# First adder convolution: three near slots and a gathered list per 32 positions, in place of four slots and one list per 128

## The chip, the cores and the metric

The kernel runs on one core of a Trainium2 chip. A core has a matrix engine (TensorE, "PE" in the profile, with its weight loads listed apart as "PEld"), a vector engine (VectorE, "DVE"), an activation engine (ScalarE, "ACT"), a general engine (GpSimd, "POOL") and a queue engine that starts most transfers (SyncE, "SP"). Each engine works through its own list of instructions in order and waits on semaphores for the others.

The metric is the device time of one execution in microseconds. It was 13987.03 us before the change, the median of three runs (13982.17 to 13997.77). One further execution was recorded by the profiler: 13941.95 us, with a span of 13939.6 us from its first to its last instruction.

## The reference, cut to what matters

The whole computation is four layers on an image batch of 4 x 128 x 64 x 64. The change lies in layer 1, in the first of its two adder convolutions:

```python
def adder_conv(x, w):                 # 3x3, stride 1, pad 1
    patches = lax.conv_general_dilated_patches(x, (3, 3), (1, 1), [(1, 1), (1, 1)])
    p = patches.reshape(N, Ck, H * W)                  # Ck = 128 * 9
    def per_channel(wc):
        return -jnp.sum(jnp.abs(p - wc[None, :, None]), axis=1)
    out = lax.map(per_channel, w.reshape(Cout, Ck))
    ...
out = adder_conv(shift_conv(x, w_shift1), w_add1)
out = relu(batchnorm(out))
out = adder_conv(shift_conv(out, w_shift2), w_add2)
```

So every output is a sum of 1152 absolute differences between values y of the shift convolution and weights w. Layer 0 (an attention over 4096 positions) comes before it, layers 2 and 3 after it.

## The kernel before

**What is summed.** An absolute difference is rewritten as |y - w| = 2 relu(w - y) + y - w. For one input channel and one position the term 2 relu(w - y) is a row of 1152 numbers (9 taps x 128 output channels). If y lies above all weights of the channel, the row is zero. If it lies below all of them ("below"), the row is linear in w and y. Only in between ("near") must the row be formed. For each group of 128 positions (there are 128 groups, numbered m; four of them make a block q of 512 positions) the rows are summed over channels into a 128 x 1152 tile `t` of three PSUM banks:

- `add_linear` (L600): nine bf16 matmuls for the "below" values, three for each bank.
- Near slots: in every window of 32 positions, slot l holds for each channel its l-th near position. `distance` forms r = relu(w + at) for the 128 channels, 128 x 1152, on VectorE (L575) or ScalarE (L573), taking turns. `add_near` (L585) multiplies it by a one-hot matrix `hot_n` of 32 columns. The four windows g of a group go to the four 32-column strips of the array; there are 12 such matmuls for a slot, and an f32 matmul is two records in the profile. `S_NEAR` is 4.
- The list: near values that found no slot are listed for the whole group, up to 8 for a channel (`TOP`) and up to 128 in all, each in a seat (a partition) of its own. An indirect DMA on GpSimd's queue, `weights_of` (L522), gathers for each seat the weight row of its channel (128 rows of 4608 bytes) into a tile `wl` of the pool `gp` (three buffers). One `distance` and one `add_far` (L592, three matmuls of 128 columns) add it.
- A group whose list overflows is marked in `crowded` and left to `sparse_rest`, a loop whose number of passes is read from the data. The trace before holds no instruction of this loop's own lines (L808, L815).

**Closing.** `closed` (L610) copies the three banks out on ScalarE to `tsa`; `combine` (L633) adds them into the output with shift matmuls on TensorE. Both are issued one group late: after slot l = 1 of the next group.

**Preparing the next block.** While the groups of block q are summed, a generator `found(q + 1)` prepares block q + 1 in small steps. Its parts in order: the shift convolution (L297, nine taps, with the casts of L288 and L289 for the block after), `ranks` (L418 to L427), `totals` (matmuls of L557, result read by VectorE at L564), `slots` (L538 to L542), and `listed`: counts (L451 to L461), two matmuls for the seats (L464, L465), `max` and `max_index` for each stretch (L468, L469), `chairs` (a 0/1 matrix of seats, L480), the fields `what` (L485 to L495), the list matmuls (L500), eight empty steps (`AFTER`), and `value`, `lanes`, `hot` (L508 to L515). After every `distance` a call of `beside` advances the generator by 88 / 68 steps (68 distances in a block).

**What sets the order.** Nearly all these instructions are held in the program's order (`keep_in_program_order`), so the order of the emission is the order on each engine. What may run ahead is set by buffers: r has six for VectorE (`r0`) and six for ScalarE (`r1`), and PSUM has five banks for `t`, three of which a group takes.

Of the kernel before, what the change touches and what calls it, by code (L numbers as in the profile page):

```python
# [9 lines left out]
F32 = mybir.dt.float32  # L10
BF16 = mybir.dt.bfloat16
# [3 lines left out]
ALU = mybir.AluOpType  # L15
AX = mybir.AxisListType
# [3 lines left out]
P = 128  # L20
# [5 lines left out]
BK = 512  # L26
# [273 lines left out]
        ))  # L300


S_NEAR, TOP, FIELDS = 4, 8, 5
AFTER = 8
FAR = 2.0 ** 100
GROUPS = BK // P
# [3 lines left out]
class Sparse:  # L310
# [85 lines left out]
    def pools(self, ctx, r_bufs):  # L396
        def pool(name, bufs, **kw):
            return ctx.enter_context(self.tc.tile_pool(name=f"{self.tag}{name}", bufs=bufs, **kw))

        self.tp = pool("t", 1)  # L400
        self.kp = pool("q", 2)
        self.rp = pool("r", r_bufs)
        self.lp = pool("l", 1)
        self.gp = pool("g", 3)
        self.op = pool("o", 2)
        self.ps_t = pool("pt", 5, space=PSUM)
        self.ps_o = pool("po", 2, space=PSUM)
        self.ps_c = pool("pc", 1, space=PSUM)
        self.banks = {}
        self.begun = set()  # L410
        self.evacuated = {}
# [30 lines left out]
    def listed(self, q, v, near, counts):  # L442

        nc, then, u = self.tc.nc, self.tc.keep_in_program_order, f"{self.tag}{q}"
        small, data = [P, GROUPS], [P, GROUPS, TOP]

        def new(shape, name, dtype=F32):
            return self.lp.tile(shape, dtype, tag=name, name=f"{name}{u}")

        away = self.tp.tile([P, BK], F32, tag="t1", name=f"away{u}")  # L450
        then(nc.vector.tensor_scalar(away, near, S_NEAR + 0.5, -FAR, ALU.is_lt, ALU.mult))  # L451
        yield
        masked = self.tp.tile([P, BK], F32, tag="t3", name=f"masked{u}")
        then(nc.vector.tensor_tensor(masked, away, v, ALU.add))
        yield
        count = new(small, "count")
        then(nc.vector.tensor_reduce(count, away.rearrange("p (j k) -> p j k", k=P), AX.X, ALU.add))
        then(nc.vector.tensor_scalar(count, count, 1.0 / FAR, float(P), ALU.mult, ALU.add))
        full = new(small, "full")
        then(nc.vector.tensor_scalar(full, count, float(TOP), 1000.0, ALU.is_gt, ALU.mult))  # L460
        then(nc.vector.tensor_tensor(full, full, count, ALU.add))  # L461
        yield
        pb = self.ps_c.tile([P, 2, GROUPS], F32, tag="cv", name=f"pbase{u}")
        then(nc.tensor.matmul(pb[:, 0, :], self.before, full, start=True, stop=False, skip_group_check=True))  # L464
        then(nc.tensor.matmul(pb[:, 1, :], self.cm.ones, full, start=False, stop=True, skip_group_check=True))  # L465
        at, where = new(data, "at8"), new(data, "where", U32)
        for j in range(GROUPS):
            then(nc.vector.max(at[:, j, :], masked[:, bass.ts(j, P)]))  # L468
            then(nc.vector.max_index(where[:, j, :], at[:, j, :], masked[:, bass.ts(j, P)]))  # L469
            yield  # L470
            yield
        crowded = self.crowded[:, GROUPS * q : GROUPS * (q + 1)]
        then(nc.vector.tensor_scalar(crowded, pb[:, 1, :], float(P), None, ALU.is_gt))
        base = new(small, "base")
        then(nc.vector.scalar_tensor_tensor(base, crowded, 1000.0, pb[:, 0, :], ALU.mult, ALU.add))
        then(nc.vector.tensor_tensor(counts[:, GROUPS * q : GROUPS * (q + 1)], crowded, count, ALU.mult))
        yield
        wide = [P, GROUPS, TOP + P]
        chairs = self.lp.tile(wide, BF16, tag="chairs", bufs=2, name=f"chairs{u}")
        then(nc.vector.tensor_tensor(  # L480
            chairs, self.chair.unsqueeze(1).broadcast_to(wide), base.unsqueeze(2).broadcast_to(wide), ALU.is_equal
        ))
        yield
        valid = new(data, "valid")
        then(nc.vector.tensor_scalar(valid, at, -FAR / 2, None, ALU.is_gt))  # L485
        then(nc.vector.tensor_tensor(at, at, valid, ALU.mult))
        what = new([*data, FIELDS], "what", BF16)
        then(nc.vector.tensor_copy(what[..., 0], at))
        yield
        then(nc.vector.tensor_tensor(at, at, what[..., 0], ALU.subtract))  # L490
        then(nc.vector.tensor_copy(what[..., 1], at))
        then(nc.vector.tensor_tensor(what[..., 2], at, what[..., 1], ALU.subtract))
        yield
        then(nc.vector.scalar_tensor_tensor(what[..., 3], where, 1.0, valid, ALU.add, ALU.mult))
        then(nc.vector.tensor_scalar(what[..., 4], valid, self.lane, None, ALU.mult))  # L495
        yield
        pl = self.ps_c.tile([P, GROUPS, FIELDS], F32, tag="cv", name=f"plist{u}")
        for j in range(GROUPS):
            for l in range(TOP):
                then(nc.tensor.matmul(  # L500
                    pl[:, j, :], chairs[:, j, TOP - l : TOP - l + P], what[:, j, l, :], start=(j + l == 0),
                    stop=(j == GROUPS - 1 and l == TOP - 1), skip_group_check=True,
                ))
            yield
        for _ in range(AFTER):
            yield
        value, of = self.kp.tile(small, F32, tag="value", name=f"value{u}"), new([P, GROUPS, 2], "of")
        then(nc.vector.tensor_reduce(value, pl[:, :, 0:3], AX.X, ALU.add))  # L508
        then(nc.vector.tensor_copy(of, pl[:, :, 3:5]))
        lanes = self.kp.tile(small, I32, tag="lanes", name=f"lanes{u}")  # L510
        then(nc.vector.tensor_copy(lanes, of[:, :, 1]))
        yield
        hot = self.kp.tile([P, GROUPS, P], F32, tag="hotl", name=f"hotl{u}")
        for j in range(GROUPS):
            then(nc.vector.tensor_scalar(hot[:, j, :], self.place, of[:, j, 0:1], 2.0, ALU.is_equal, ALU.mult))  # L515
        yield
        yield value, lanes, hot

# [124 lines left out]
def sparse_adder(tc, cm, sp, x_d, wqs, stats, counts, p_d, y_d, tag):  # L643
# [7 lines left out]
    nc = tc.nc  # L651
    then = tc.keep_in_program_order
    with ExitStack() as ctx:
# [76 lines left out]
            pass  # L730
        groups = blocks * GROUPS
        waiting = None
        per = (S_NEAR * 4 + 1) * GROUPS

        ripe = []

        def combined(m, t, total):
            b, n = divmod(m, N // P)
            sp.combine(b, n, sp.closed(t, m, total))
            ripe.extend([AFTER, b, k] for k in sp.done(n))  # L740

        steps, due = iter(()), 0.0
        for m in range(groups):
            q, j = divmod(m, GROUPS)
            if j == 0:
                for _ in steps:
                    pass
                below, total, hot_n, at_n, value, lanes, hot_l = ready.pop(q)
                steps = found(q + 1) if q + 1 < blocks else iter(())

            def beside(of):
                nonlocal due
                for waits in list(ripe):
                    waits[0] -= 1
                    if waits[0] == 0:
                        finished(*waits[1:])
                        ripe.remove(waits)
                due += of * 88.0 / per
                while due >= 1.0:
                    due -= 1.0  # L760
                    next(steps, None)

            t = sp.open_rows(m)
            weights = sp.weights_of(lanes[:, j : j + 1], m)
            sp.add_linear(t, below[:, bass.ts(j, P)])
            for l in range(S_NEAR):
                rs = []
                for g in range(4):
                    w = 4 * j + g
                    rs.append(sp.distance(g % 2 == 1, at_n[:, l, w : w + 1], f"n{m}_{l}_{g}"))  # L770
                    beside(1)
                sp.add_near(t, lambda g: hot_n[:, l, P * j + 32 * g : P * j + 32 * g + 32], lambda g: rs[g], False)
                if l == 1 and waiting is not None:
                    combined(*waiting)
            r = sp.distance(m % 2 == 1, value[:, j : j + 1], f"l{m}", weights)
            beside(1)
            sp.add_far(t, hot_l[:, j, :], r, False, True)
            waiting = (m, t, total[:, j : j + 1])
        combined(*waiting)
        for _, b, k in ripe:  # L780
# [1945 lines left out]
```

## Time and profile before

| what | before |
|---|---|
| median of three runs | 13987.03 us |
| profiled execution, its time and its span | 13941.95 us, 13939.6 us |
| TensorE, VectorE, ScalarE, GpSimd busy over the span | 91%, 77%, 66%, 31% |
| first adder convolution, from the first group to the last result | 2050 to 4238 us |
| in it TensorE, VectorE, ScalarE, GpSimd busy, of 2188 us | 2114, 1479, 1519, 180 us |
| granted TensorE clock in it | 0.99 |
| one block of four groups (two successive first gathers, 2994.32 to 3062.97 us) | 68.65 us |

A row of a group of instructions gives line, engine and operation, the tile written and the tiles read, their shapes and how many there were; after the bar the busy time and the mean of one; after the second bar how long the engine was idle just before them and who ended that. A row of the timeline gives start and length in us, with the idle time before it in square brackets. A row of the windows gives, for a stretch of time, the busy time and number of instructions of TensorE, its weight loads, VectorE, ScalarE and GpSimd, then the granted clock, the share of the DMA engines and GB/s.

### The profile page before, as it was taken

The numbers are of one execution on the slowest core, as the hardware profiler recorded it, in microseconds if no ns is written. First come the engines' busy times: TensorE is split into PE (matmuls) and PEld (weight loads), VectorE is DVE, ScalarE is ACT, GpSimd is POOL, SyncE is SP. The second block draws the span as 40 slices with busy tenths as digits, with TensorE's granted clock in tenths as the row PEclk, the third lists the DMA queues.
The fourth block names the chain that finished last, engine by engine and source line by source line (L and its number), as shares of the span: only waits on it lengthen the run. The fifth ranks groups of instructions, "written<-read, shape, count | busy, mean of one in ns | idle before, by whom it ended". The sixth has DMA issues, their size and how long they took to land. (4 is left out here: it accounts for less than half of the span.)

```text
span 13939.6 us, 217437 instructions
## 1 busy us (share of the span) xinstructions
PE 12715.4 (91%) x85293; PEld 5605.6 (40%) x85320; DVE 10711.0 (77%) x15704; ACT 9244.1 (66%) x10490; POOL 4389.7 (31%) x2328
## 2 busy tenths in 40 slices
PE   9999989999996999999999999997788869899998
PEld 4444434444443334334533454444233223333332
DVE  7778876666664778777777778875786689999997
ACT  5666646666664788877787778884333456676676
POOL 5666640000001001001000100001000159999997
PEclk9999989999997999999999999998887679999999
DMA  0000001111111101101100211114110368999997
GB/s 17 10 5 11 5 22 47 47 49 49 48 45 47 37 33 39 38 27 59 61 30 24 71 55 51 52 54 124 19 17 35 123 205 235 247 255 254 252 256 200
DMA packets 388839, 1134.70 MB, mean 81 GB/s; under 512 B 143317, under 2 KB 171792, under 8 KB 315980
## 3 DMA queue, kind: packets, MB, share of 16 engines
q1 hardware_dynamic: 322332, 857.60, 21.1%
q0 software_dynamic: 65312, 260.86, 6.2%
q8 instruction: 676, 11.08, 0.3%
q14 instruction: 375, 3.07, 0.1%
q10 hardware_dynamic: 144, 2.10, 0.0%
HBM read 910.21 MB, written 202.38 MB: 80 GB/s over the span
## 5 line engine op out<-in xcount | busy, mean ns | idle before, releaser
L573 ACT ACTIVATE ra<-a2wa,vc 128x1152 f32<-128x1152 f32 x2397 | 2875.6, 1250 | 661.8 <-PE ta L1264 648.2
L1264 PE MATMUL ta<-ra,a2pick 128*32 128x384 f32 x33024 | 3174.1, 494 | 104.6 <-DVE ra L575 63.8
L575 DVE TENSOR_SCALAR ra<-a2wa,vc 128x1152 f32<-128x1152 f32 x3107 | 2425.3, 818 | 766.6 <-PE ta L1264 751.6
L2387 PE MATMUL mg<-h,ident 128*128 128x512 f32 x4096 | 1957.8, 616 | 206.6 <-ACT m L2396 168.5
L1264 PEld LDWEIGHTS ta<-ra,a2pick 128*32 128x32 f32 x33024 | 1310.0, 110 | 1623.2 <-issue 852.2
L2372 DVE TENSOR_TENSOR_SCAN h<-da,h,dbu 128x1024 f32<-128x1024 f32 x768 | 1804.4, 2349 | 128.8 <-ACT da L2358 37.4
L573 ACT ACTIVATE ra1n<-a1wa,atna 128x1152 f32<-128x1152 f32 x1024 | 1227.2, 1248 | 601.5 <-PE ta L585 584.7
L2387 PEld LDWEIGHTS mg<-h,ident 128*128 128x128 f32 x4096 | 727.7, 191 | 1438.4 <-ACT m L2396 690.1
L190 POOL TENSOR_TENSOR ssum<-ssum,et 128x512 f32<-128x512 f32 x960 | 1228.8, 1280 | 233.3 <-ACT et L185 166.6
L2400 POOL TENSOR_TENSOR m<-m,C 128x2048 f32<-128x2048 f32 x256 | 1157.1, 4532 | 102.0 <-ACT m L2396 81.6
L2351 POOL TENSOR_TENSOR dbu<-du,B 128x2048 f32<-128x2048 f32 x256 | 1157.2, 4535 | 100.1 <-DMA B<-xdbl_d 45.1
L575 DVE TENSOR_SCALAR ra1n<-a1wa,atna 128x1152 f32<-128x1152 f32 x1024 | 806.3, 814 | 419.7 <-PE ta L585 400.7
L585 PE MATMUL ta<-ra1n,hotna 128*32 128x384 f32 x12288 | 1089.4, 489 | 12.9 <-DVE ra1n L575 12.9
L522 POOL DMA_INDIRECT wla<-in_w_add,lanes x156 | 173.9, 1115 | 2940.6 <-DVE lanes L1235 1375.5
L1264 PE MATMUL ta<-ra,hot 128*32 128x384 f32 x10368 | 1046.9, 498 | 53.9 <-ACT ra L573 36.1
L153 PE MATMUL pe<-q,k 128*128 128x512 f32 x2048 | 1051.1, 596 | 8.7 <-DVE mx L163 8.1
L196 PE MATMUL pav<-et,vT 128*128 128x512 f32 x2048 | 1042.0, 593 | 1.5 <-ACT et L185 1.5
L573 ACT ACTIVATE ra<-a2wa,at 128x1152 f32<-128x1152 f32 x793 | 944.4, 1248 | 131.8 <-PE ta L1264 125.4
L155 ACT COPY et<-pe 128x512 f32<-128x512 f32 x1024 | 595.4, 581 | 592.3 <-PE pe L153 575.7
L163 DVE TENSOR_TENSOR mx<-pe,mx 128x512 f32<-128x512 f32 x992 | 679.6, 685 | 336.0 <-ACT et L155 332.9
L575 DVE TENSOR_SCALAR ra<-a2wa,at 128x1152 f32<-128x1152 f32 x935 | 728.9, 817 | 224.8 <-PE ta L1264 221.1
L2358 ACT ACTIVATE da<-dl,af 128x1024 f32<-128x1024 f32 x512 | 572.6, 1118 | 420.5 <-DVE h L2372 325.7
(486 smaller groups left out, 16692.2 us busy)
## 6 DMA issues: line engine op xcount, KB each, us to landing
dl<-delta_d SPq DMA_DIRECT2D x256, 512.0 KB
dl<-delta_d SPq DMA_DIRECT2D x512, 256.0 KB
du<-du_d SPq DMA_DIRECT2D x256, 512.0 KB
du<-du_d SPq DMA_DIRECT2D x512, 256.0 KB
taps_d<-tsa SPq DMA_DIRECT2D x82, 576.0 KB
sz_d<-sz SPq DMA_DIRECT2D x64, 256.0 KB
xs_d<-xs SPq DMA_DIRECT2D x8, 2048.0 KB
delta_d<-dv SPq DMA_DIRECT2D x32, 512.0 KB
```

The source lines that it names most:

```text
L153: nc.tensor.matmul(pe, k[:, bass.ts(j, P)], unit[u, "q"], start=True, stop=True)
L163: nc.vector.tensor_tensor(mx, pe, mx, ALU.max)
L190: nc.gpsimd.tensor_tensor(unit[u, "sum"], unit[u, "sum"], at, ALU.add)
L196: nc.tensor.matmul(unit[u, "av"], image[u // NB][2][:, j, :], at, start=(j == 0), stop=(j == NJ - 1))
L573: then(nc.scalar.activation(r, w, AF.Relu, bias=at))
L575: then(nc.vector.tensor_scalar(r, w, at, 0.0, ALU.add, ALU.max))
L585: self.tc.keep_in_program_order(self.tc.nc.tensor.matmul(t[y][32 * g : 32 * g + 32, :], lhs(g), rhs(g)[:, bass.ts(y, TC)], start=first, st ...
L1264: self.tc.keep_in_program_order(self.tc.nc.tensor.matmul(t[y][32 * g : 32 * g + 32, :], lhs, r[:, bass.ts(y, TC)], start=first, stop=False ...
L2351: then(nc.gpsimd.tensor_tensor(t, du, by_states(tiles[n][0], 0, h), ALU.mult))
L2372: then(nc.vector.tensor_tensor_scan(t[:, cols][:, s], da[:, s], st[n, "dbu", h][:, cols][:, s], 0.0 if e % 4 == 0 else st["last"], ALU.mul ...
L2387: then(nc.tensor.matmul(pm, cm.ident, st[n, way, h][:, bass.ts(k, BK)], start=(way == 0), stop=(way == 1)))
L2400: then(nc.gpsimd.tensor_tensor(m, m, by_states(tiles[n][0], 1, h), ALU.mult))
```

## The change

The near slots go from four to three. The list is made for each window of 32 positions in place of each 128: a block has 16 lists (`WINDOWS`) of up to 128 seats in place of four. Each group gathers four weight tiles in place of one, forms four distances from them (two on each engine), and adds them with `add_near`, in the form of a slot, in place of `add_far`. The gather pool has six buffers in place of three; `chairs` has one in place of two. `beside` advances the generator by 104 / 64 steps (64 distances in a block). `crowded` is still kept for each group of 128: a group is marked if any of its four lists overflows.

```diff
@@ -300,7 +300,8 @@
         ))
 
 
-S_NEAR, TOP, FIELDS = 4, 8, 5
+S_NEAR, TOP, FIELDS = 3, 8, 5
+WINDOWS = BK // 32
 AFTER = 8
 FAR = 2.0 ** 100
 GROUPS = BK // P
@@ -401,7 +402,7 @@
         self.kp = pool("q", 2)
         self.rp = pool("r", r_bufs)
         self.lp = pool("l", 1)
-        self.gp = pool("g", 3)
+        self.gp = pool("g", 6)
         self.op = pool("o", 2)
         self.ps_t = pool("pt", 5, space=PSUM)
         self.ps_o = pool("po", 2, space=PSUM)
@@ -442,7 +443,7 @@
     def listed(self, q, v, near, counts):
 
         nc, then, u = self.tc.nc, self.tc.keep_in_program_order, f"{self.tag}{q}"
-        small, data = [P, GROUPS], [P, GROUPS, TOP]
+        small, data, groups = [P, WINDOWS], [P, WINDOWS, TOP], [P, GROUPS]
 
         def new(shape, name, dtype=F32):
             return self.lp.tile(shape, dtype, tag=name, name=f"{name}{u}")
@@ -454,29 +455,35 @@
         then(nc.vector.tensor_tensor(masked, away, v, ALU.add))
         yield
         count = new(small, "count")
-        then(nc.vector.tensor_reduce(count, away.rearrange("p (j k) -> p j k", k=P), AX.X, ALU.add))
-        then(nc.vector.tensor_scalar(count, count, 1.0 / FAR, float(P), ALU.mult, ALU.add))
+        then(nc.vector.tensor_reduce(count, away.rearrange("p (w k) -> p w k", k=32), AX.X, ALU.add))
+        then(nc.vector.tensor_scalar(count, count, 1.0 / FAR, 32.0, ALU.mult, ALU.add))
         full = new(small, "full")
         then(nc.vector.tensor_scalar(full, count, float(TOP), 1000.0, ALU.is_gt, ALU.mult))
         then(nc.vector.tensor_tensor(full, full, count, ALU.add))
         yield
-        pb = self.ps_c.tile([P, 2, GROUPS], F32, tag="cv", name=f"pbase{u}")
+        pb = self.ps_c.tile([P, 2, WINDOWS], F32, tag="cv", name=f"pbase{u}")
         then(nc.tensor.matmul(pb[:, 0, :], self.before, full, start=True, stop=False, skip_group_check=True))
         then(nc.tensor.matmul(pb[:, 1, :], self.cm.ones, full, start=False, stop=True, skip_group_check=True))
         at, where = new(data, "at8"), new(data, "where", U32)
-        for j in range(GROUPS):
-            then(nc.vector.max(at[:, j, :], masked[:, bass.ts(j, P)]))
-            then(nc.vector.max_index(where[:, j, :], at[:, j, :], masked[:, bass.ts(j, P)]))
-            yield
+        for w in range(WINDOWS):
+            then(nc.vector.max(at[:, w, :], masked[:, bass.ts(w, 32)]))
+            then(nc.vector.max_index(where[:, w, :], at[:, w, :], masked[:, bass.ts(w, 32)]))
             yield
         crowded = self.crowded[:, GROUPS * q : GROUPS * (q + 1)]
-        then(nc.vector.tensor_scalar(crowded, pb[:, 1, :], float(P), None, ALU.is_gt))
+        most, of_group = new(groups, "most"), new(groups, "of_group")
+        then(nc.vector.tensor_reduce(most, pb[:, 1, :].rearrange("p (j w) -> p j w", w=4), AX.X, ALU.max))
+        then(nc.vector.tensor_scalar(crowded, most, float(P), None, ALU.is_gt))
+        then(nc.vector.tensor_reduce(of_group, count.rearrange("p (j w) -> p j w", w=4), AX.X, ALU.add))
+        then(nc.vector.tensor_tensor(counts[:, GROUPS * q : GROUPS * (q + 1)], crowded, of_group, ALU.mult))
+        yield
         base = new(small, "base")
-        then(nc.vector.scalar_tensor_tensor(base, crowded, 1000.0, pb[:, 0, :], ALU.mult, ALU.add))
-        then(nc.vector.tensor_tensor(counts[:, GROUPS * q : GROUPS * (q + 1)], crowded, count, ALU.mult))
-        yield
-        wide = [P, GROUPS, TOP + P]
-        chairs = self.lp.tile(wide, BF16, tag="chairs", bufs=2, name=f"chairs{u}")
+        then(nc.vector.scalar_tensor_tensor(
+            base.rearrange("p (j w) -> p j w", w=4), crowded.unsqueeze(2).broadcast_to([P, GROUPS, 4]), 1000.0,
+            pb[:, 0, :].rearrange("p (j w) -> p j w", w=4), ALU.mult, ALU.add,
+        ))
+        yield
+        wide = [P, WINDOWS, TOP + P]
+        chairs = self.lp.tile(wide, BF16, tag="chairs", bufs=1, name=f"chairs{u}")
         then(nc.vector.tensor_tensor(
             chairs, self.chair.unsqueeze(1).broadcast_to(wide), base.unsqueeze(2).broadcast_to(wide), ALU.is_equal
         ))
@@ -494,25 +501,30 @@
         then(nc.vector.scalar_tensor_tensor(what[..., 3], where, 1.0, valid, ALU.add, ALU.mult))
         then(nc.vector.tensor_scalar(what[..., 4], valid, self.lane, None, ALU.mult))
         yield
-        pl = self.ps_c.tile([P, GROUPS, FIELDS], F32, tag="cv", name=f"plist{u}")
-        for j in range(GROUPS):
+        pl = self.ps_c.tile([P, WINDOWS, FIELDS], F32, tag="cv", name=f"plist{u}")
+        for w in range(WINDOWS):
             for l in range(TOP):
                 then(nc.tensor.matmul(
-                    pl[:, j, :], chairs[:, j, TOP - l : TOP - l + P], what[:, j, l, :], start=(j + l == 0),
-                    stop=(j == GROUPS - 1 and l == TOP - 1), skip_group_check=True,
+                    pl[:, w, :], chairs[:, w, TOP - l : TOP - l + P], what[:, w, l, :], start=(w + l == 0),
+                    stop=(w == WINDOWS - 1 and l == TOP - 1), skip_group_check=True,
                 ))
-            yield
+            if w % 2:
+                yield
         for _ in range(AFTER):
             yield
-        value, of = self.kp.tile(small, F32, tag="value", name=f"value{u}"), new([P, GROUPS, 2], "of")
+        value, of = self.kp.tile(small, F32, tag="value", name=f"value{u}"), new([P, WINDOWS, 2], "of")
         then(nc.vector.tensor_reduce(value, pl[:, :, 0:3], AX.X, ALU.add))
         then(nc.vector.tensor_copy(of, pl[:, :, 3:5]))
         lanes = self.kp.tile(small, I32, tag="lanes", name=f"lanes{u}")
         then(nc.vector.tensor_copy(lanes, of[:, :, 1]))
         yield
-        hot = self.kp.tile([P, GROUPS, P], F32, tag="hotl", name=f"hotl{u}")
-        for j in range(GROUPS):
-            then(nc.vector.tensor_scalar(hot[:, j, :], self.place, of[:, j, 0:1], 2.0, ALU.is_equal, ALU.mult))
+        hot = self.kp.tile([P, WINDOWS, 32], F32, tag="hotl", name=f"hotl{u}")
+        then(nc.vector.tensor_tensor(
+            hot, self.place[:, 0:32].unsqueeze(1).broadcast_to([P, WINDOWS, 32]), of[:, :, 0:1].broadcast_to([P, WINDOWS, 32]),
+            ALU.is_equal,
+        ))
+        yield
+        then(nc.vector.tensor_tensor(hot, hot, hot, ALU.add))
         yield
         yield value, lanes, hot
 
@@ -730,7 +742,7 @@
             pass
         groups = blocks * GROUPS
         waiting = None
-        per = (S_NEAR * 4 + 1) * GROUPS
+        per = (S_NEAR * 4 + 4) * GROUPS
 
         ripe = []
 
@@ -755,13 +767,13 @@
                     if waits[0] == 0:
                         finished(*waits[1:])
                         ripe.remove(waits)
-                due += of * 88.0 / per
+                due += of * 104.0 / per
                 while due >= 1.0:
                     due -= 1.0
                     next(steps, None)
 
             t = sp.open_rows(m)
-            weights = sp.weights_of(lanes[:, j : j + 1], m)
+            weights = [sp.weights_of(lanes[:, w : w + 1], f"{m}_{w}") for w in range(4 * j, 4 * j + 4)]
             sp.add_linear(t, below[:, bass.ts(j, P)])
             for l in range(S_NEAR):
                 rs = []
@@ -772,9 +784,12 @@
                 sp.add_near(t, lambda g: hot_n[:, l, P * j + 32 * g : P * j + 32 * g + 32], lambda g: rs[g], False)
                 if l == 1 and waiting is not None:
                     combined(*waiting)
-            r = sp.distance(m % 2 == 1, value[:, j : j + 1], f"l{m}", weights)
-            beside(1)
-            sp.add_far(t, hot_l[:, j, :], r, False, True)
+            rs = []
+            for g in range(4):
+                w = 4 * j + g
+                rs.append(sp.distance(g % 2 == 1, value[:, w : w + 1], f"l{m}_{g}", weights[g]))
+                beside(1)
+            sp.add_near(t, lambda g: hot_l[:, 4 * j + g, :], lambda g: rs[g], False)
             waiting = (m, t, total[:, j : j + 1])
         combined(*waiting)
         for _, b, k in ripe:
```

## The prediction

> **What bounds the kernel now.** I read the windows of the first adder convolution first, then its groups of instructions, then the timeline of one block on TensorE, VectorE and ScalarE.
>
> The windows:
>
> ```profile
> 2050.00:4238.00 2188.00, 2114.31 (x19060) 1088.99 (x19058) 1479.29 (x2896) 1518.91 (x1527) 180.14 (x164) 0.99 0.15 47
> 3018.00:3087.00 69.00, 66.43 (x607) 34.28 (x603) 46.93 (x92) 47.73 (x48) 5.56 (x5) 1.00 0.16 48
> ```
>
> TensorE is busy 97% of the stage and 66.4 of the 69 us of one block, VectorE 47 us, ScalarE 48 us. So on average TensorE is the bound, with 22 us of room on VectorE. The groups:
>
> ```profile
> L585 PE MATMUL ta<-ra1n,hotna 128*32 128x384 f32 x12288 | 1089.4, 489 | 12.9 <-DVE ra1n L575 12.9
> L592 PE MATMUL ta<-ra1l,hotla 128*128 128x384 f32 x768 | 281.9, 503 | 0.0
> L500 PE MATMUL plista<-whata,chairsa 128*128 128x5 bf16 x1024 | 35.3, 166 | 3.9 <-DVE whata L495 3.9
> L480 DVE TENSOR_TENSOR chairsa<-a1chair,basea 128x544 bf16<-128x544 f32 x32 | 23.2, 725 | 0.0
> L1164 DVE MAX8 at<-masked 128x8 f32<-128x32 f32 x508 | 94.6, 186 | 0.0
> ```
>
> A near slot costs TensorE 1089.4 / 512 = 2.1 us (four slots, 128 groups), the list of a group 281.9 / 128 = 2.2 us. The last row is of the second adder convolution: the search on 32 positions exists there.
>
> An average hides what happens inside a block. TensorE, then VectorE, then TensorE again:
>
> ```profile
> 3035.04 0.95 PE L557 MATMUL ptota<-one_col,spa 128*128 128x1 f32 x8
> ...
> 3054.22 2.13 PE L585 MATMUL ta<-ra1n,hotna 128*32 128x384 f32 x20 [0.48 <-DVE ra1n L575]
> 3056.28 2.27 PE L633 MATMUL oa<-a1shift,tsa 128*128 128x128 f32 x18
> 3058.39 0.55 PE L500 MATMUL plista<-whata,chairsa 128*128 128x5 bf16 x16
> ...
> 3077.31 2.20 PE L592 MATMUL ta<-ra1l,hotla 128*128 128x384 f32 x6
> 3079.35 0.49 PE L600 MATMUL ta<-a1w,belowa 128*128 128x384 bf16 x2
> 3081.94 1.30 PE L600 MATMUL ta<-a1w,belowa 128*128 128x384 bf16 x7 [2.10 <-ACT tsa L610]
> ```
>
> ```profile
> 3036.10 0.16 DVE L564 COPY totala<-ptota 128x4 f32<-128x4 f32 x1 [3.65 <-PE ptota L557]
> ...
> 3057.94 0.26 DVE L495 TENSOR_SCALAR whata<-valida,a1lane 128x32 bf16<-128x32 f32 x1
> ```
>
> VectorE may not run ahead at will: once a block, at L564, it waits for TensorE. From there to the last field at L495 it works without a pause, 3036.10 to 3058.1, **22.0 us**; in this stretch lie ten distances and nearly all preparation of the next block. TensorE's list matmuls need that last field, and start at 3058.39, 0.3 us later. So every block has a chain: totals on TensorE, VectorE's stretch, list matmuls, and TensorE again to the next totals. Before, TensorE has just about as much work beside the stretch (it waits some 1 us in it). This chain is what the change has to be read against.
>
> **The change part by part.** Durations are start-to-start distances in the timeline of the profiled execution (13941.95 us; the median of the runs, 13987, is 0.3% above it, and I add the difference to the median).
>
> *TensorE's work.* Block before, by starts: four times linear 1.46, four slots 8.1 and list 2.04; combines 2.2 + 2.9 + 2.8 + 2.1; convolution 6.1; totals 0.9; seats 0.4; list matmuls 32 at 16 in 0.49 = 1.0: 64.8 us, and with the wait of 2.1 for ScalarE and some 1.5 for VectorE the 68.65 us of a block. After: three slots and a list that is a fourth slot (12 matmuls of the same form), so 4 x 2.04 = 8.2 less; list matmuls 128 in place of 32, 3.9 in place of 1.0. Sum 59.5 us. If TensorE stayed the bound, a block would gain 5.3 us.
>
> *VectorE's stretch from L564 to the last field.* In the order of the changed kernel there are again ten distances in it, and the 1.36 us of the finished output (L723, L726). Removed: one one-hot (0.34) and one product (0.60) of the fourth slot, and half of a reduction (1.14 to 0.61): -1.5 us. Added:
> - Search: 16 pairs of `max` and `max_index` on 32 positions. In the second convolution a pair takes 0.40 us from start to start (6001.93, next instruction 6002.33), so 6.4; before, four on 128 positions at 0.60 (3050.85 to 3051.45), 2.4. So +4.0.
> - `chairs` 128x2176 in place of 128x544: 0.725 us and 1632 elements more at 1.02 ns (between L454's 512 in 0.692 and L542's 1024 in 1.215): 2.39, +1.7.
> - Eight operations for the fields on 128 in place of 32 elements: 8 x 96 x 1.02 ns = +0.8.
> - Two reductions by group and one product more: +0.4 at some 0.2 each.
>
> Sum 22.0 + 5.4 = **27.4 us**. TensorE's work beside it, in the new order: list 2.04, linear 1.46, two slots 4.0, combine 2.8, seats 0.4, slot 2.0, list 2.04, linear 1.46, slot 2.0 = 18.3 us. Then come the first 16 list matmuls, which the change puts ahead of the second slot of the third group. So TensorE stands some 9 us in a block, about 6 us of it in one piece before these.
>
> *TensorE from the list matmuls to the next totals.* Ten slots (lists among them) 20.2, two linear 2.9, three combines 7.2, convolution 6.1, list matmuls 3.9, totals 0.9 = 41.2 us.
>
> *The wait for ScalarE.* Third-bank matmuls of a group (the row at 3081.94) need the first bank of the group before copied out (L610), and ScalarE does that after its four distances for the first two slots. With six `r1` buffers and eight distances a group, the last two of these four can only start when TensorE has begun the list: 0.2 + 2 x 1.16 + 0.58 = 3.1 us after its start, while TensorE wants the bank 2.3 us after it. So 0.8 us more at a boundary; before, the list took no `r1` tile or one, four slots lay between, so at most one distance was left there and nothing was waited for, save at a block's start. There the two casts (L288, 0.7 each) and VectorE's subtraction between them (0.85) lie in front: 5.4 after the start, 3.1 us of wait against 2.1. On this part of the chain: one boundary 0.8, one block start 3.1: 3.9 us. Bounds: 2.1 (as now) and 4.5.
>
> *The clock.* After an idle time TensorE runs slower:
>
> ```profile
> 4308.95 1.48 PE L297 MATMUL pca<-x3a,a2wq 128*128 128x512 bf16 x6
> ...
> 4314.87 3.57 PE L297 MATMUL pca<-x3a,a2wq 128*128 128x512 bf16 x8 [3.29 <-ACT va L942]
> ```
>
> Before 3.29 us of idle a matmul took 0.23 us from start to start, after it 0.45; the loss until the pace is back was some 2 us. After the 2.10 us at 3081.94 there was none (seven in 1.30). So an idle of 6 us a block costs up to 2.3, of 3.1 perhaps the same. I take 1.5; bounds 0 and 4.6. [...]
>
> *The gathers.* 512 in place of 128 on POOL's queue, four a group: 4 x 1.3 = 5.3 us of a group's 17, on an engine busy 180 of 2188 us. Behind them lie only the memsets of inputs two blocks on. With six buffers the third gather of a group waits for the first list distance of the group before, and is used about one group later (14 us or more); landing takes 4.7 to 6.0 us now, and 4.6 to 9.2 in the second convolution, which sends four together. Waited for: 0; the rival below prices it. SP's queue keeps its transfers.
>
> *Block and sum.* 0.1 + 27.4 + 41.2 + 3.9 + 1.5 = 74.1 us against 68.65: **+5.4 us**. 31 blocks have a preparation beside them: +167. The first preparation stands alone: +5.4 on VectorE, +2.9 on TensorE: +8. The last block has none: 4 x (0.8 - 2.04) = -5. Sum **+170 us**: 14112 in a profile, 14157 against the median; I say 14155.
>
> **The rivals.**
> - *TensorE stays the bound; faster.* VectorE's average room would do: 47 + 6 us of 62. A block would be 59.5 + 2.1 to 3.9 of waits, 62 to 63.5 us, -160 to -210 us: 13,780 to 13,830. It needs VectorE's stretch no longer than the 18.3 us (about 19 with a boundary wait) beside it. The point of balance: 68.65 - 41.2 - 3.9 - 0.1 = 23.4 us without a clock loss; above that it is slower. I have 27.4, and the six-deep buffers cannot help, since L564 takes the lead away just before. Only if the pairs of search came much cheaper in a row would it fall there.
> - *Balance.* The stretch 1 us shorter, waits for ScalarE as now, no clock loss: 5.4 - 1 - 1.8 - 1.5 = +1.1 a block, +37 us: 14,024. A little more, and nothing is measurable.
> - *Gathers late.* If landing and issue went to 9.2 + 4 x 1.6 = 15.6 us against some 14 available, 1.6 us in each of 128 groups: +205 on top, 14,360. Against it: in the second convolution, with bursts of four, VectorE and ScalarE waited 11 us in all for these tiles to land.
> - *The lists overflow.* Then `sparse_rest` runs: a pass of four ranks takes 128 x (4 x 2.04 + 2.5) = 1.4 ms. Worked out from the reference's own inputs, the fullest window would hold 98 of 128 seats and the fullest channel 7 of 8, so it should not.
>
> **How the numbers follow.** A difference under 0.2% (28 us) is about what a measurement of this kernel can't tell from no change. Chances: my case 0.80, TensorE bound 0.08, balance 0.06, late gathers 0.04, overflow 0.02. Faster 0.08, within 0.2% 0.06, slower 0.86. Range of my case: low from the balance sum, 14,020; high with 4.6 of clock loss, 4.5 of waits and 0.5 more on VectorE, 5.4 + 3.1 + 0.6 + 0.5 = +9.6 a block, +300: 14,290. Beyond it lie the faster case, half of the balance and the last two: under 0.2.
>
> **What the profile would show.** Right: in the first convolution TensorE's busy share falls from 97% to some 82%, its list matmuls wait for the last field about 6 us a block, L564's successor still waits for the totals, the block lasts 73 to 75 us, 128x2176 takes 2.4 us, and a wait for the evacuated bank stands at each boundary outside the stretch. Wrong: TensorE above 95% with blocks near 62 us (VectorE kept up), or waits for the gathered tiles, or instructions of the rest loop. The prediction fails most easily by VectorE's stretch, where 4 us decide the sign.

## The result, and the profile after

The changed kernel takes 14244.12 us (median of four runs, 14222.0 to 14273.67) against 13992.4 us of the kernel before beside it: a ratio of 1.0181, 95% interval 1.0167 to 1.0196. It is slower by some 252 us. The forecast was slower by 170 us, 14155 in a range of 14020 to 14290.

All of it lies in the first adder convolution. From VectorE's first reading of the totals to the first matmul that prepares the second convolution it took 2238.6 us before and 2499.6 after, 261 us more. (The two profiled executions differ by 298; the one of before, 13941.95 us, was some 50 us faster than the median of its runs, and the other stages make up the rest.) A block, taken as the mean of the 31 intervals between successive readings of the totals, went from 67.77 to **75.97 us**. (The first interval is short in both, 36.09 and 42.35 us; the 30 behind it have 68.82 and 77.09 in the mean.)

The windows of the stage and of one block, after (busy time and instructions of TensorE, its weight loads, VectorE, ScalarE, GpSimd; then granted clock, DMA share, GB/s):

```profile
2050.00:4504.00 2454.00, 2097.45 (x21386) 1049.54 (x21386) 1610.27 (x3898) 1427.39 (x1464) 595.64 (x548) 0.92 0.41 135
3007.40:3084.50 77.10, 66.42 (x675) 32.87 (x672) 50.92 (x124) 44.78 (x47) 18.64 (x18) 0.91 0.41 135
```

TensorE is busy 85% of the stage in place of 97%, and no engine took its place as the bound: VectorE has 66%, ScalarE 58%. The granted clock fell from 0.99 to 0.92. The timeline of TensorE in that block, after, shows where the idle time is:

```profile
3006.26 1.05 PE L569 MATMUL ptota<-one_col,spa 128*128 128x1 f32 x8
...
3035.17 0.57 PE L507 MATMUL plista<-whata,chairsa 128*128 128x5 bf16 x16 [6.23 <-DVE whata L502]
3035.68 3.92 PE L597 MATMUL ta<-ra1n,hotna 128*32 128x384 f32 x24
...
3048.77 1.82 PE L612 MATMUL ta<-a1w,belowa 128*128 128x384 bf16 x9
...
3064.23 2.40 PE L612 MATMUL ta<-a1w,belowa 128*128 128x384 bf16 x7 [2.98 <-ACT tsa L622]
3066.42 5.86 PE L297 MATMUL a1pc<-a1x,a1wq 128*128 128x512 bf16 x18
```

Three things are to be seen. The list matmuls wait 6.23 us for the last field. The slot behind them takes 3.92 us, where a slot took 2.1 before. At the block start the third bank is waited for 2.98 us, and then seven linear matmuls take 2.40 us (1.30 before) and 18 of the convolution 5.86 (15 took 3.44 before, so 18 some 4.1). The convolution before, at the same place of a block:

```profile
3083.07 3.44 PE L297 MATMUL a1pc<-a1x,a1wq 128*128 128x512 bf16 x15
```

The same block of the changed kernel on VectorE:

```profile
3007.42 0.16 DVE L576 COPY totala<-ptota 128x4 f32<-128x4 f32 x1 [0.69 <-PE ptota L569]
...
3029.32 2.43 DVE L487 TENSOR_TENSOR chairsa<-a1chair,basea 128x2176 bf16<-128x2176 f32 x1
...
3034.70 0.42 DVE L502 TENSOR_SCALAR whata<-valida,a1lane 128x128 bf16<-128x128 f32 x1
```

From the totals at 3007.42 to the end of the last field at 3035.12 VectorE works 27.7 us without a pause; before, the same stretch was 22.0.

### The profile page after: what moved, and what is told of

The parts are those of the page before. It is cut to its first block, busy times and chain, and to the rows that moved or that the text cites. A ratio compares the mean times of both kernels' runs of the same rounds, so it can differ in the third digit from the quotient of the medians.

```text
span 14238.1 us, 223859 instructions
## 1 busy us (share of the span) xinstructions
PE 12718.5 (89%) x87597; PEld 5554.7 (39%) x87624; DVE 10846.3 (76%) x16728; ACT 9158.1 (64%) x10426; POOL 4805.1 (34%) x2712
## 5 line engine op out<-in xcount | busy, mean ns | idle before, releaser
L585 ACT ACTIVATE ra1n<-a1wa,atna 128x1152 f32<-128x1152 f32 x768 | 924.2, 1249 | 712.1 <-PE ta L597 680.0
L534 POOL DMA_INDIRECT wla<-in_w_add,lanesa x512 | 591.0, 1154 | 1887.5 <-ACT ra1l L585 1021.6
L597 PE MATMUL ta<-ra1n,hotna 128*32 128x384 f32 x9216 | 890.9, 517 | 28.1 <-DVE ra1n L587 28.1
```

Source lines behind the costliest of these rows:

```text
L534: self.tc.nc.gpsimd.indirect_dma_start(w, None, self.w_rows, bass.IndirectOffsetOnAxis(ap=lanes, axis=0))
L585: then(nc.scalar.activation(r, w, AF.Relu, bias=at))
L597: self.tc.keep_in_program_order(self.tc.nc.tensor.matmul(t[y][32 * g : 32 * g + 32, :], lhs(g), rhs(g)[:, bass.ts(y, TC)], start=first, st ...
```

## The experiments

Three theories were tested. A: the chain of totals, VectorE's stretch and list matmuls sets the block, and the idle time it leaves on TensorE makes TensorE slow afterwards. B: four times the gathers slow the stage. C: the slow clock has another cause than idle time. All ratios are against the kernel before, run beside; a block is the mean of the 31 intervals, from one profile.

| kernel | ratio, 95% interval | block, us |
|---|---|---|
| before | 1 | 67.77 |
| the changed kernel | 1.0181, 1.0167 to 1.0196 | 75.97 |
| e1 search twice | 1.0369, 1.0352 to 1.0386 | 83.82 |
| e2 no gather | (see there) | 75.36 |
| e3 close early | 1.0068, 1.0051 to 1.0085 | 70.62 |
| e4 fill idle | 1.0141, 1.0124 to 1.0158 | 73.74 |
| e5 spread | 1.0089, 1.0072 to 1.0106 | 71.36 |
| e6 spread, early | 1.0009, 0.9999 to 1.0018 | 67.82 |
| e7 early, fill | 1.0032, 1.0020 to 1.0045 | 69.07 |
| e8 before, early | 0.9944, 0.9928 to 0.9961 | 65.15 |
| e9 wide, early | 0.9887, 0.9871 to 0.9904 | 62.65 |
| e10 wide, early, ScalarE | 0.9888, 0.9871 to 0.9904 | 62.69 |

### e1: the search twice

```diff
-            then(nc.vector.max(at[:, w, :], masked[:, bass.ts(w, 32)]))
-            then(nc.vector.max_index(where[:, w, :], at[:, w, :], masked[:, bass.ts(w, 32)]))
+            for _ in range(2):
+                then(nc.vector.max(at[:, w, :], masked[:, bass.ts(w, 32)]))
+                then(nc.vector.max_index(where[:, w, :], at[:, w, :], masked[:, bass.ts(w, 32)]))
```

> The changed kernel with every pair of max and max_index issued twice, with the same results: 16 more pairs, 6.4 us more work on VectorE in each block, and nothing else. Theory A (the chain: totals on TensorE, VectorE's stretch, list matmuls): the stretch is on the path, so all of it shows, 6.4 us in each of 31 blocks and in the first preparation, +205 us, 14,450. Theory B (four times the gathers slow the stage): VectorE is busy 55 of 76 us of a block, the extra work finds room, 0 us, 14,244. Theory T (TensorE's own work bounds the stage): 0 us as well.

Measured: 14489.7 us against 13975.17, +3.69% where the changed kernel has +1.81%; a block is 7.85 us longer. VectorE, busy on average two thirds of the time, hid none of it. That the step is 7.85 and not 6.4 has a reason in the timeline of VectorE in this kernel:

```profile
3018.18 0.16 DVE L577 COPY totala<-ptota 128x4 f32<-128x4 f32 x1 [0.69 <-PE ptota L570]
...
3028.12 0.18 DVE L470 MAX8 at8a<-maskeda 128x8 f32<-128x32 f32 x1
...
3028.64 0.20 DVE L470 MAX8 at8a<-maskeda 128x8 f32<-128x32 f32 x1
...
3029.05 0.17 DVE L470 MAX8 at8a<-maskeda 128x8 f32<-128x32 f32 x1
...
3053.87 0.42 DVE L503 TENSOR_SCALAR whata<-valida,a1lane 128x128 bf16<-128x128 f32 x1
```

A pair followed by one that writes the same tile again takes 0.52 us from start to start, one followed by another window's 0.41. The stretch is 36.1 us, 8.4 longer, of which the extra pairs at 0.52 are 16 x 0.52 = 8.3. So VectorE's stretch is on the path, and theory A holds in this point.

### e2: no gather

```diff
-            weights = [sp.weights_of(lanes[:, w : w + 1], f"{m}_{w}") for w in range(4 * j, 4 * j + 4)]
+            weights = [None] * 4
```

> The changed kernel without any gather in the first adder convolution: the list distances take the resident weight tile, so the list's terms are formed from other weights than the listed channels' and the computation is changed in that part; number, shape and order of all other instructions stay. Theory A: the gathers are hidden, 14,244 within 25 us. Theory B: most of the 252 us goes with them, 13,990 to 14,100.

The whole kernel took 23895.76 us, which was not foreseen and says nothing on the gathers: with other values in the first convolution the second one's own overflow loop runs (its tiles, `ra2rest` and `ta2rest`, appear only in this trace). The stage itself can be compared, since its instructions but for the gathers are the same. Its window in this kernel:

```profile
2050.00:4500.00 2450.00, 2093.02 (x21386) 1048.80 (x21386) 1613.86 (x3912) 1430.47 (x1468) 18.86 (x34) 0.92 0.04 13
```

GpSimd falls from 596 to 19 us and the DMA share from 0.41 to 0.04, and the stage from the first totals takes 2478.6 us against 2499.6; a block takes 75.36 against 75.97, and the granted clock is 0.92 as it was. Theory B falls: without all gathers the stage is 21 us shorter, a twelfth of the loss. Since a profile is one execution, how much of these 21 us the gathers are is left open.

### e3: the copies out of PSUM one slot earlier

```diff
         def combined(m, ts):
             b, n = divmod(m, N // P)
             sp.combine(b, n, ts)
...
+                if l == 0 and waiting is not None:
+                    m0, t0, total0 = waiting
+                    waiting = (m0, sp.closed(t0, m0, total0))
                 if l == 1 and waiting is not None:
                     combined(*waiting)
```

> The changed kernel with ScalarE's copies out of PSUM (closed) issued after the first slot of the next group in place of after its second, so that at most the distances of one slot stand before them; the combine stays where it is. Theory A with the clock tied to idle time: the wait of 3.4 us at each block start goes (106 us in all), and with it the slow matmuls behind it (18 of the convolution in 5.86 us against 4.1, seven linear ones in 2.4 against 1.14: 3.0 us a block, 96 us): -200 us, 14,045. If the slow pace has another cause than the idle time (theory C): -106 us, 14,140. Theory B: 0 us.

Measured: 14069.59 us, +0.68%: of 1.81% more than half is gone, and a block is 5.35 us shorter. TensorE at the block start in this kernel:

```profile
3057.22 2.12 PE L597 MATMUL ta<-ra1l,hotla 128*32 128x384 f32 x24
3059.27 1.64 PE L612 MATMUL ta<-a1w,belowa 128*128 128x384 bf16 x9
3060.74 4.09 PE L297 MATMUL a1pc<-a1x,a1wq 128*128 128x512 bf16 x18
```

No wait, nine linear matmuls in 1.64 us, and 18 of the convolution in 4.09 in place of 5.86. Over the stage the linear matmuls' busy time falls from 250 to 211 us and the convolution's from 239 to 204: 75 us, or 2.4 us a block, beside some 106 us of wait. These matmuls were not touched; only the idle time ahead of them was taken away. That is against theory C at this place. The gain falls short of the 200 expected (some 160): the slow pace behind a block start was 2.4 us a block in the mean and not 3.0.

### e4: the idle time before the list matmuls filled

```diff
+        idle = self.ps_c.tile([P, BK], F32, tag="cv", name=f"idle{u}")
+        for _ in range(24):
+            then(nc.tensor.matmul(idle, self.w3[0][:, 0:P], self.w3[0][:, 0:BK], start=True, stop=True))
         yield
         wide = [P, WINDOWS, TOP + P]
```

> The changed kernel with 24 bf16 matmuls of 128x512 whose result nobody reads, into the small PSUM bank, issued on TensorE as soon as VectorE has read the seats: 5.5 us of work that lies in the idle time of some 6.2 us before the list matmuls. Clock tied to idle time (theory A): the slot after the list matmuls takes 2.1 us again in place of 3.9 and the combine behind it 2.1 in place of 2.3, -2 us in each of 31 blocks, -60 us, 14,180. Theory C (slow for another cause, load or transfers): no gain, 0 to +20 us.

Measured: 14172.23 us, +1.41%; a block is 2.23 us shorter, although TensorE does 24 matmuls more in it. TensorE in this kernel:

```profile
3072.43 5.34 PE L486 MATMUL idlea<-a1w 128*128 128x512 bf16 x24 [0.40 <-DVE basea L480]
3078.28 0.56 PE L510 MATMUL plista<-whata,chairsa 128*128 128x5 bf16 x16 [0.51 <-DVE whata L505]
3078.77 2.14 PE L600 MATMUL ta<-ra1n,hotna 128*32 128x384 f32 x24
3080.84 2.27 PE L648 MATMUL oa<-a1shift,tsa 128*128 128x128 f32 x18
3082.95 2.57 PE L510 MATMUL plista<-whata,chairsa 128*128 128x5 bf16 x96
3085.45 3.10 PE L600 MATMUL ta<-ra1n,hotna 128*32 128x384 f32 x24
```

The list matmuls start as late after VectorE's last field as before, but the slot behind them takes 2.14 us in place of 3.92, and so in all 31 blocks. Work that nobody needs makes the kernel faster, since the time it fills was lost anyway and the pace behind it is kept. So the slow pace of this slot comes from the idle time ahead of it; theory C falls here. Not every slow slot goes: the one behind the other 96 list matmuls takes 3.10 us with no idle time ahead of it. It is slow in 22 of the 31 blocks (in the changed kernel in none), some 29 us in all; the last section comes back to it.

### e5 and e6: VectorE's stretch spread over more of the block

e5 issues the same preparation in more and smaller steps; e6 adds the early copies of e3.

```diff
             then(nc.vector.max_index(where[:, w, :], at[:, w, :], masked[:, bass.ts(w, 32)]))
             yield
+            yield
...
-        then(nc.vector.tensor_tensor(
-            chairs, self.chair.unsqueeze(1).broadcast_to(wide), base.unsqueeze(2).broadcast_to(wide), ALU.is_equal
-        ))
-        yield
+        half = [P, WINDOWS // 4, TOP + P]
+        for i in range(4):
+            of4 = slice(WINDOWS // 4 * i, WINDOWS // 4 * (i + 1))
+            then(nc.vector.tensor_tensor(
+                chairs[:, of4, :], self.chair.unsqueeze(1).broadcast_to(half),
+                base[:, of4].unsqueeze(2).broadcast_to(half), ALU.is_equal,
+            ))
+            yield
+            yield
...
-                due += of * 104.0 / per
+                due += of * 136.0 / per
```

One or two empty steps more stand in the slots, the counts and the fields too.

> The changed kernel with the same work in more and smaller steps: two steps a pair in the search, one or two more in slots, counts and fields, chairs in four pieces, and 136 in place of 104 steps a block, so that VectorE's stretch from the totals to the last field holds 16 distances in place of ten, some 32 us, beside some 30 us of TensorE's work. Theory A: the wait before the list matmuls falls from 6.2 us to under 2, and the slow slot behind it goes: -6 to -8 us in each of 31 blocks, 14,000 to 14,060; the wait at the block start stays. If VectorE's work as such, not its place, were the cost: 14,244.

> The two edits together: the steps spread as in the run before, and the copies out of PSUM after the first slot. Theory A: both waits gone, a block comes to TensorE's own work of 59.5 us and 2 to 3 us, against 67.8 before the change: -150 to -190 us against the kernel before, 13,790 to 13,840. If TensorE's work had been underestimated in the prediction's sum, it stays above 65 us a block, 13,900 or more.

Measured: e5 14099.47 us, +0.89%, a block 4.6 us shorter than in the changed kernel, where 6 to 8 were expected. e6 13986.57, +0.09%, not told apart from the kernel before; expected was a gain of 150 or more. TensorE in e6 shows why:

```profile
3047.25 0.61 PE L467 MATMUL pbasea<-fulla,a1before 128*128 128x16 f32 x2 [2.69 <-DVE fulla L463]
...
3048.22 4.07 PE L611 MATMUL ta<-ra1n,hotna 128*32 128x384 f32 x24
...
3071.98 1.76 PE L519 MATMUL plista<-whata,chairsa 128*128 128x5 bf16 x64 [2.15 <-DVE whata L514]
3073.67 3.29 PE L611 MATMUL ta<-ra1l,hotla 128*32 128x384 f32 x24
```

The wait of 6.2 us became two, of 2.7 us for the counts and 2.2 for the fields, and behind each a slot is slow again. VectorE's stretch took 33.2 us, 32 were expected, and TensorE had less work beside it than was reckoned. The expectation failed; spreading had not gone far enough, or only moved the wait. The runs e9 and e10 tell which. The rival that stood in e6's expectation, that TensorE's work had been underestimated, is excluded by the 62.65 us of e9.

### e7: early copies and filled idle time together

The edits of e3 and e4 in one kernel.

> The changed kernel with the early copies and the 24 unread matmuls together: both cold starts gone, VectorE's stretch left as it is. If the two effects add as they did alone (5.35 and 2.2 us a block), a block takes 68.4 us, 0.6 us more than before: +20 us against the kernel before, 13,990 to 14,010. If the slow clock has one cause that either edit alone removes, more remains: 14,050.

Measured: 14021.68 us, +0.32% (0.20 to 0.45), a block of 69.07 us against 68.4 if both effects added up in full. Of 5.35 + 2.23 = 7.58 us a block they give 6.90 together, so they overlap by 0.7 us: alone, either also kept some of the other's matmuls fast (in e4 the convolution fell from 239 to 222 us). With both of these idle times gone or filled, the changed kernel is still slower than before: what is left is VectorE's stretch itself, and a slow slot behind the 96 list matmuls in 15 of the 31 blocks, some 21 us in all.

### e8: the early copies in the kernel before

The edit of e3, in the kernel before.

> The kernel before the change with only the early copies. Its wait of 2.1 us at each block start goes: -60 to -70 us, 13,915; no slow matmuls stood behind that wait, so nothing more. If that wait was covered otherwise: 0.

Measured: 13893.26 us, 0.56% faster (0.39 to 0.72), 2.6 us a block. The wait for ScalarE was a cost before the change as well. It is a little more than the wait of 2.1 us, and the granted clock shows where the other 0.5 is from: in the kernel before it is at half in nine stretches of 3.4 us, each at one of these waits, and in e8 in none. Half of these 31 us is 15 us, 0.5 us a block.

### e9 and e10: spread further

e9 takes e6, with the nine convolution taps in five steps, three steps for a pair of the search, one more before the fields, and the list matmuls in four steps in place of eight. e10 also gives ScalarE one distance more in two of four groups.

```diff
                 shifted(tc, pc, wqs, here, t)
-                yield
+                if t % 2:
+                    yield
+            yield
...
             then(nc.vector.max_index(where[:, w, :], at[:, w, :], masked[:, bass.ts(w, 32)]))
             yield
             yield
+            yield
...
-            if w % 2:
+            if w % 4 == 3:
                 yield
```

```diff
-                    rs.append(sp.distance(g % 2 == 1, at_n[:, l, w : w + 1], f"n{m}_{l}_{g}"))
+                    rs.append(sp.distance(g % 2 == 1 or (g == 2 and l == 2 and j in (1, 2)), at_n[:, l, w : w + 1], f"n{m}_{l}_{g}"))
```

> As the run with spread steps and early copies, but spread further: the nine taps of the convolution in five steps, three steps a pair in the search, the list matmuls in four steps, so that VectorE's stretch holds 21 distances, some 36 us, beside some 36 us of TensorE's work. Theory A: the two waits left in the narrower spread (2.7 us for the counts, 2.2 us for the fields) and the slow matmuls behind them go, 5 to 7 us a block: 62 to 63 us a block against 67.8 before the change, 13,790 to 13,840. If those waits only move to another place of the block: 13,970 again.

> The same, and in the second and third group of each block one more distance (window 2 of the third slot) is formed on ScalarE in place of VectorE: 1.5 us less in VectorE's stretch, 2.3 us more on ScalarE, which has room. Theory A: up to 1.5 us a block better than the run before where VectorE's stretch still ends last (-45 us), the same where TensorE is already the bound.

Measured: e9 13776.61 us against 13932.95, a ratio of 0.9887 (0.9871 to 0.9904), a block of 62.65 us. The changed kernel is now faster than the one before, and also than e8 (0.9944). The stage and the list matmuls in e9:

```profile
2050.00:3977.00 1927.00, 1869.76 (x20312) 994.14 (x20316) 1530.76 (x3837) 1364.89 (x1388) 594.05 (x525) 0.98 0.49 163
```

```profile
L521 PE MATMUL plista<-whata,chairsa 128*128 128x5 bf16 x4096 | 108.7, 166 | 11.1 <-DVE whata L516 11.1
```

TensorE is busy 97% of the time, and the list matmuls wait 11 us in the whole stage in place of 204. A wait of about 1.5 us a block for the counts stays. e10 is the same within its interval: 1.5 us less on VectorE bring nothing any more, as TensorE is the bound again. So it is not the amount of VectorE's work that made the change slow, but that the work stood in one piece between two things that TensorE needed.

## Why the prediction was right

The direction, the mechanism and most of the terms held. One term, the clock, was taken too small, and one wait that was counted did not come.

- **The chain.** VectorE's stretch was put at 27.4 us and took 27.7, and the wait before the list matmuls, "about 6 us of it in one piece", took 6.23. `chairs` took 2.43 us for 2.39. e1 showed that the stretch is on the path, e9 that the loss goes when it is spread.
- **TensorE's own work.** It was summed to 59.5 us a block. With both waits gone a block takes 62.65 us in e9, with some 1.5 us of wait for the counts and some slow slots left. No run took all waits away, so the sum itself is borne out only so far.
- **The wait for ScalarE.** 3.1 us were expected at the block start; 2.98 and 3.73 stand in the two blocks looked at, 102 us over 31 places in the stage. The 0.8 us at the other boundary is not there: nine linear matmuls took 1.82 us at 3048.77, with no wait shown. Sixteen list matmuls stand ahead of that list in the new order and give ScalarE half a microsecond more; that is argued from the order, no run tried it.
- **The clock: the term that was too small.** "So an idle of 6 us a block costs up to 2.3, of 3.1 perhaps the same. I take 1.5; bounds 0 and 4.6." It cost some 4. The linear matmuls took 34 us more than before in the stage, the convolution 23, the combine 10, and the slot behind the list matmuls some 3.9 in place of 2.1 in 31 blocks, 55: 122 us, 3.9 a block. The granted clock says the same: from 2060 us to the last result it is at half for 379 us in place of 31, and TensorE is busy in 288 and 31 of them, so that by estimate (half of the busy time) 144 us are lost in place of 15. The mechanism was named and its upper bound held, but 1.5 is less than the price the prediction gave to one of the two idle times. Taking away either idle time took its part of the slow matmuls away (e3: 75 us of linear and convolution matmuls; e4: 2.23 us a block). With 27.7 us for the stretch, 3.9 for the clock and the boundary's 0.8 left out, the sum is 0.1 + 27.7 + 41.2 + 3.1 + 3.9 = 76.0 us; measured 75.97. That they meet so closely is luck: against the 77.09 us of the 30 full intervals the sum is 1 us short.
- **The edges.** The last block was to gain 5 us. From the last totals to the second convolution it took 144.6 us against 137.8, so it lost 7; with the early copies of e3, 140.9. The 12 us between forecast and measurement are one twentieth of the loss, and were not looked into.
- **The rivals.** TensorE as the bound, the faster case, is what e9 reaches, through the order of the steps and not through cheaper search. Late gathers are excluded by e2, overflow by the trace: no instruction of the rest loop stands between the last group and the second convolution.

That 170 stood in place of 252 us is thus mostly the clock: 2.4 us in each of 31 intervals, 74 us. The boundary wait that did not come takes 25 us back, VectorE's stretch adds 9 and the last block 12. That is 70 of the 82 us; the rest is open.

## What to carry to other kernels

An average share of 66% busy on the second engine says nothing if its work stands in one piece between two points where the first engine waits: add up each engine's work between such points, from the timeline, and compare the two sums. If the sums differ, spread the work over more of the loop before doubting the change itself; here nearly the same instructions in another order, with ScalarE's copies earlier, went from 1.8% slower to 1.1% faster. Half of the 1.1% is not the change's own: the early copies alone made the kernel before 0.56% faster (e8). And price an idle time on TensorE with what comes behind it (here a slot of 3.92 us in place of 2.1 behind 6.23 us of idle time, and by e3 2.4 us a block behind the wait at the block start), for every idle time of the loop, not only for the longest one.

## What was not expected of the hardware

- **Whether a wait of 2 to 3 us slows TensorE depends on where it falls.** After 2.98 us of waiting in the changed kernel the seven linear matmuls took 2.40 us, and the convolution behind them was slow as well. In e4 the same wait of 2.97 us is followed by both paces:

```profile
2957.67 2.40 PE L615 MATMUL ta<-a1w,belowa 128*128 128x384 bf16 x7 [2.97 <-ACT tsa L625]
...
3033.04 1.30 PE L615 MATMUL ta<-a1w,belowa 128*128 128x384 bf16 x7 [2.97 <-ACT tsa L625]
```

The granted clock tells them apart. In these traces it is either full or half, and its changes lie on a fixed grid of 3.41 us. Here are the two windows of this grid that hold the first wait and the matmuls behind it, then the two that hold the second (in each row, TensorE's busy time stands first behind the length, and the granted clock third from the end):

```profile
2953.37:2956.78 3.41, 1.33 (x14) 0.34 (x7) 2.13 (x3) 2.50 (x4) 0.00 (x0) 1.00 0.87 314
2956.78:2960.19 3.41, 2.52 (x8) 1.13 (x8) 1.55 (x3) 3.41 (x6) 0.00 (x0) 0.50 0.13 51
3028.46:3031.87 3.41, 1.61 (x18) 0.47 (x11) 2.13 (x4) 2.50 (x4) 0.00 (x0) 1.00 0.93 362
3031.87:3035.29 3.42, 2.25 (x13) 1.19 (x13) 1.84 (x3) 3.42 (x6) 0.00 (x0) 1.00 0.03 12
```

Where one window holds most of the wait, TensorE is busy for 1.33 of its 3.41 us, and the clock is at half in the next window. Where two windows share the wait, busy 1.61 and 2.25 us, it stays full. In the stage of the changed kernel each of the 59 falls to half comes after a window with TensorE busy at most 0.44 of it, and no window at full clock below that is without a fall. Waits of 2.1 us do it too: of the 29 at the block starts of the kernel before, nine were followed by half the clock, though not the one that the prediction looked at. There the windows ahead of the falls have TensorE busy for at most 1.32 of 3.41 us, 0.39, and two of 1.38 (0.41) and one of 1.48 (0.43) had no fall behind them: no one busy share parts the windows in both kernels.

- **A run of tiny matmuls was followed by slow ones in 13 of 31 blocks.** In e9 the 128 list matmuls of 128x5 stand in one run of 3.39 us without a gap, and in 13 of the 31 blocks the slot behind them took 3.1 to 4.1 us, in the others 2.14. Two blocks of it in e9's timeline of TensorE:

```profile
3061.26 3.39 PE L521 MATMUL plista<-whata,chairsa 128*128 128x5 bf16 x128
3064.58 3.57 PE L613 MATMUL ta<-ra1n,hotna 128*32 128x384 f32 x24
...
3125.33 3.39 PE L521 MATMUL plista<-whata,chairsa 128*128 128x5 bf16 x128
3128.64 2.14 PE L613 MATMUL ta<-ra1n,hotna 128*32 128x384 f32 x24
```

The same run of matmuls is followed by both paces, and over the stage the slow slots cost 16 us. In e4 the granted clock fits with these matmuls counting as idle time. If the list, seat and totals matmuls are left out of TensorE's busy time, each of the 42 falls in its stage comes after a window of the grid that is busy at most 0.43, and every other window at full clock is busy at least 0.44; with them counted, some falls come after windows that are busy all through. In e9 the falls come after 0.41 and less in the same way, with three windows below that and no fall. In the changed kernel the clock does not fit: three windows that are busy all through, 2.2 to 2.3 of their 3.41 us with list matmuls, are busy 0.38 to 0.41 without them, under the 0.44 of the falls, and the clock stays full behind them. So whether these matmuls count as idle time is not shown. No experiment was made on it.
